# Routing tokens to experts in four groups of blocks instead of once, in a fused Mamba-and-MoE kernel

## The chip, the cores and the metric

The kernel runs on one core of a Trainium2 chip. The metric is the device time of one execution, in microseconds (us); lower is better. The core has a matrix engine (TensorE, PE in the profile), three engines for elementwise work (VectorE or DVE, ScalarE or ACT, GpSimd or POOL), and a synchronisation engine (SyncE or SP) whose queue issues most of the transfers. Each engine works through its own list of instructions strictly in order and waits on semaphores for the others.

## The reference

For x of shape 2 x 2048 x 256 (4096 tokens) the reference computes `x + s * silu(m)`, where `xn = layernorm(x)`:

```
s = mamba block of xn:
    xz = rmsnorm(xn) @ in_proj.T ; xp, z = split(xz)
    xc = silu(causal_conv4(xp))                      # 512 channels
    dt, B, C = parts of xc @ x_proj.T                # 16 states
    h[t] = h[t-1] * exp(dt*A) + dt*xc*B ;  y = sum_states(h*C) + xc*D
    s1 = xn + (y * silu(z)) @ out_proj.T
    s  = s1 + silu(rmsnorm(s1) @ w1.T) @ w2.T        # dense MLP
m = mixture of 8 experts on xn, the best 2 of each token:
    gate = softmax(xn @ gate_w + gate_b); top-2
    m = sum over 2 of gate_k * (relu(xn @ w1[e] + b1[e]) @ w2[e] + b2[e])
```

All of it is float32. The two best experts of a token are known only from the data, so tokens must be sorted to experts at run time.

## The kernel before

The 4096 tokens are cut into 8 blocks of 512 (`NBLK`), a block into 4 rows of 128 tokens (`J`), so that there are `NI` = 32 rows of tokens. The opening of the kernel goes over all blocks; after it one long loop runs the scan, and all other work is drawn into that loop.

**Opening.** `moments(b)` takes means and variances of a block on VectorE (L215, L216). `factors(g)` turns those of a pair of blocks (`GB` = 2) into scales with a ping-pong between VectorE and ScalarE (L193 to L233). `norm(b)` forms `xr` (for the gate and the mamba block) on ScalarE (L243), transposes it on TensorE (L258), and forms `xn`, the rows that the experts need, half on VectorE (L262) and half on ScalarE (L267). `logits(b)` copies the transposed block out of PSUM, one half on ScalarE (L278) and one on VectorE (L279), stores it to DRAM, and multiplies with the gate's weights (L287) into `lgp`. The loop issues norm(b) ahead of logits(b-1).

`gate_and_route()` then runs once, for all 32 rows: on VectorE it scales the logits (L309), picks the two best experts (L319 to L329), counts with two matmuls how many tokens go to each expert ahead of each token (L348, L350), and computes for each token and choice a slot, that is a row in the DRAM buffer `xs_d`, where each expert begins at a multiple of 256 rows (L384 to L386). It also finds for each of the 39 tiles of 256 slots (`NTILE`) which expert owns it (`expert_of`, L396). After it 64 indirect transfers issued by GpSimd scatter the rows of xn to their slots (L1019). Between two of them stands a small copy on ScalarE into the tile `turn` (L1030). `xs_d` was filled with zeros by one transfer of 9,984 KB near the start (L186), since a tile may be only partly used.

`front(c)` makes the inputs of the scan for block c: projection on TensorE (`px`, L474), convolution taps and silu (ScalarE L484 to L507, VectorE L499 and L512), projection to dt, B and C (L520, L537), softplus for dt. B and C go to DRAM (`bcd`, L527) and are loaded back broadcast over all partitions (`load_bc`, L613). The tiles of B and C take over the buffers of x and of xn, so a C load waits for the scatters of one block. front(0) runs in the opening.

**Main loop.** It has 256 steps: block c, group d of 128 channels, pair g of states. In a step VectorE multiplies `b` (L1193) and makes two scans (L1197), ScalarE makes the exponentials for two steps ahead (L1088), GpSimd multiplies the last step's `h` by C (L1129), and TensorE adds `h` into `y` (L1101). There are five `h` buffers. Generators with the other work are drawn on in each step, in a fixed order of preference: the z gate, the output projection, front of the next block (`chain`), and the experts and dense MLP (`side`), which are the largest part of TensorE's work. The experts start at step 4.

An expert tile loads its rows from `xs_d` (L836), its weights by the expert's number, read into a register of SP (L826), and runs two layers (L756, L768). It stores its results to `ys_d` under the same slots (L871). The dense MLP for 256 tokens gathers the two results of each token back with four indirect transfers (L941 and its surroundings in `gather`).

Everything is issued in the order in which the Python code reaches it. No scheduler reorders it.

Of the kernel before, what the change touches and what calls it, by code (L numbers as in the profile page):

```python
# [9 lines left out]
F32 = mybir.dt.float32  # L10
# [21 lines left out]
NSLOT = NTILE * TS  # L32
NCEIL = NT // TS
LN_EPS = 1e-05
# [12 lines left out]
def kernel(  # L47
# [91 lines left out]
    one = rows.tile([P, NE * NI], F32, tag="xs", name="one")  # L139
    nc.gpsimd.memset(one, 1.0)  # L140
# [23 lines left out]
    for d in range(ND):  # L164
# [11 lines left out]
    expert_of = keep.tile([P, NTILE], mybir.dt.int32, tag="expert_of", name="expert_of")  # L176
    xnd = [spill.tile([P, J, DM], F32, tag=f"xnd{b}", name=f"xnd{b}") for b in range(NBLK)]
# [3 lines left out]
    ys_d = spill.tile([NSLOT, DM], F32, tag="ys_d", name="ys_d")  # L181


    zeros = rows.tile([P, NSLOT // P * DM // 64], F32, tag="yk", name="zeros")
    nc.gpsimd.memset(zeros, 0.0)
    nc.sync.dma_start(  # L186
        xs_d.rearrange("(p r) d -> p (r d)", p=P).rearrange("p (o n) -> p o n", o=64),
        zeros.unsqueeze(1).to_broadcast([P, 64, NSLOT // P * DM // 64]),
    )
# [20 lines left out]
    GB = 2  # L210

# [81 lines left out]
    def gate_and_route():  # L293
        def tmp3(name, shape=None):
            return hpool.tile(shape or [P, NI, NE], F32, tag="hid", name=name)

        scratch = rows.tile([P, JS * DM], F32, tag="x1", name="scratch")
        used = [0]

        def cols(name, n):  # L300
            used[0] += n
            return scratch[:, used[0] - n : used[0]]

        sh = [P, NI, NE]
        sel = [
            rows.tile(sh, F32, tag="yk", name=f"sel{k}") for k in range(TOPK)
        ]
        lg = rows.tile(sh, F32, tag="ys", name="lg")
        nc.vector.tensor_tensor(lg, lgp, unr.unsqueeze(2).to_broadcast(sh), ALU.mult)  # L309
        nc.vector.tensor_tensor(  # L310
            lg, lg, gb_sb.unsqueeze(1).to_broadcast(sh), ALU.add
        )
        top = [cols(f"top{k}", NI) for k in range(TOPK)]
        pr = tmp3("pr")
        for k in range(TOPK):
            left = lg
            if k:
                left = tmp3("left")
                nc.vector.scalar_tensor_tensor(left, sel[0], -3e38, lg, ALU.mult, ALU.add)  # L319
            nc.vector.tensor_reduce(top[k], left, AX.X, ALU.max)  # L320
            nc.vector.tensor_tensor(
                sel[k], left, top[k].unsqueeze(2).to_broadcast(sh), ALU.is_equal
            )
            nc.vector.tensor_tensor(
                sel[k], sel[k], fore.unsqueeze(1).to_broadcast(sh), ALU.mult
            )
            first = cols(f"first{k}", NI)
            nc.vector.tensor_reduce(first, sel[k], AX.X, ALU.max)
            nc.vector.tensor_tensor(  # L329
                sel[k], sel[k], first.unsqueeze(2).to_broadcast(sh), ALU.is_equal  # L330
            )
        nc.vector.tensor_tensor(
            pr, lg, top[0].unsqueeze(2).to_broadcast(sh), ALU.subtract
        )
        nc.scalar.activation(pr, pr, AF.Exp)
        tot = cols("tot", NI)
        nc.vector.tensor_reduce(tot, pr, AX.X, ALU.add)
        nc.vector.tensor_single_scalar(tot, tot, 2.0, ALU.mult)
        nc.vector.reciprocal(prob[:, 0, :], tot)
        nc.vector.tensor_sub(top[1], top[1], top[0])  # L340
        nc.scalar.activation(top[1], top[1], AF.Exp)
        nc.vector.tensor_mul(prob[:, 1, :], top[1], prob[:, 0, :])

        mask = tmp3("mask", [P, NE, NI])
        nc.vector.tensor_add(mask.rearrange("p e i -> p i e"), sel[0], sel[1])
        flat = mask.rearrange("p e i -> p (e i)")
        pe = ps_h.tile([P, NE, NI], F32, tag="h", name="pearlier")
        nc.tensor.matmul(pe.rearrange("p e i -> p (e i)"), earlier, flat, start=True, stop=True)  # L348
        pt = ps_h.tile([P, NE, NI], F32, tag="h", name="ptotal")
        nc.tensor.matmul(pt.rearrange("p e i -> p (e i)"), all1, flat, start=True, stop=True)  # L350
        tot_e = tmp3("tot_e", [P, NE, NI])
        nc.scalar.copy(tot_e, pt)

        ahead = tmp3("before_e", [P, NE, NI])
        nc.vector.tensor_tensor_scan(
            ahead.rearrange("p e i -> p (e i)"), one, tot_e.rearrange("p e i -> p (e i)"),
            0.0, ALU.mult, ALU.add,
        )
        nc.vector.tensor_sub(ahead, ahead, tot_e)

        cnt = cols("cnt", NE)
        nc.vector.tensor_reduce(cnt, tot_e, AX.X, ALU.add)
        nc.vector.tensor_single_scalar(cnt, cnt, 1.0 / TS, ALU.mult)
        over = tmp3("over", [P, NE, NCEIL])
        nc.vector.tensor_tensor(
            over, cnt.unsqueeze(2).to_broadcast([P, NE, NCEIL]),
            steps[:, 0:NCEIL].unsqueeze(1).to_broadcast([P, NE, NCEIL]), ALU.is_gt,
        )
        tiles = cols("tiles", NE)
        nc.vector.tensor_reduce(tiles, over, AX.X, ALU.add)  # L370
        upto = cols("upto", NE)
        nc.vector.tensor_tensor_scan(upto, one[:, 0:NE], tiles, 0.0, ALU.mult, ALU.add)
        base = cols("base", NE)
        nc.vector.tensor_sub(base, upto, tiles)
        nc.vector.scalar_tensor_tensor(
            base, base, float(TS), ahead[:, :, 0], ALU.mult, ALU.subtract
        )
        nc.vector.tensor_add(ahead, ahead, pe)
        nc.vector.tensor_tensor(
            ahead, ahead, base.unsqueeze(2).to_broadcast([P, NE, NI]), ALU.add  # L380
        )
        sl = cols("sl", NI)
        for k in range(TOPK):
            nc.vector.tensor_mul(sel[k], sel[k], ahead.rearrange("p e i -> p i e"))  # L384
            nc.vector.tensor_reduce(sl, sel[k], AX.X, ALU.add)
            nc.vector.tensor_copy(slot[:, k, :], sl)  # L386

        done = tmp3("done", [P, NTILE, NE])
        nc.vector.tensor_tensor(
            done, upto.unsqueeze(1).to_broadcast([P, NTILE, NE]),  # L390
            steps.unsqueeze(2).to_broadcast([P, NTILE, NE]), ALU.is_le,
        )
        own = cols("own", NTILE)
        nc.vector.tensor_reduce(own, done, AX.X, ALU.add)
        nc.vector.tensor_scalar_min(own, own, float(NE - 1))
        nc.vector.tensor_copy(expert_of, own)  # L396


# [58 lines left out]
    def bank(tag, shape, name):  # L457
        n = ring(tag, 3 if tag == "h" else 1)
        pool = ps_h if tag == "h" else ps_1
        return pool.tile(shape, F32, tag=tag, name=name), n  # L460

# [355 lines left out]
    class Expert(Ffn):  # L817
# [6 lines left out]
        def begin(self):  # L824
            i = self.i
            e = nc.sync.value_load(expert_of[0:1, i : i + 1], min_val=0, max_val=NE - 1)  # L826
            self.a1 = w1[bass.ds(e, 1)].rearrange("o d f -> (o d) f")
            self.a2 = w2[bass.ds(e, 1)].rearrange("o f d -> (o f) d")
            self.b1 = small.tile([P, NH], F32, tag="b1", name=f"b1_{i}")
            nc.sync.dma_start(self.b1, b1[bass.ds(e, 1)].rearrange("o p c -> (o p) c"))  # L830
            self.e = e

        def rows(self):
# [3 lines left out]
                self.xr, xs_d[ts(i, TS), :].rearrange("(j p) d -> p j d", p=P)  # L837
# [39 lines left out]
    class Mlp(Ffn):  # L877
# [51 lines left out]
        def gather(self):  # L929
# [9 lines left out]
            for j in range(JS):  # L939
                for k in range(TOPK):  # L940
# [3 lines left out]
                            ap=slot[:, k, i0 + j : i0 + j + 1], axis=0  # L944
                        ),
                        bounds_check=NSLOT - 1,
# [59 lines left out]
    for b in range(NBLK + 1):  # L1006
# [6 lines left out]
        if b:  # L1013
            logits(b - 1)
    gate_and_route()
    turn = small.tile([P, 1], F32, tag="turn", name="turn", bufs=1)
    for i in range(NI):
        for k in range(TOPK):
            r = nc.gpsimd.indirect_dma_start(  # L1019
                out=xs_d,  # L1020
                out_offset=bass.IndirectOffsetOnAxis(ap=slot[:, k, i : i + 1], axis=0),
                in_=xns[i // J][:, i % J, :],
                in_offset=None,
                bounds_check=NSLOT - 1,
                oob_is_err=False,
            )

            tc.declare_no_dep(r.ins, group="to_slots", reason="other rows")
            tc.add_to_no_dep_group("to_slots", r.ins)
            nc.scalar.copy(turn, zero3[:, 0:1])  # L1030
    ffns = [Expert(i) for i in range(NTILE)] + [
        Mlp(c, hf) for c in range(NBLK) for hf in range(2)
    ]
    ffns[0].begin()
    for h in range(4):
        ffns[0].load_w1(h)
        ffns[0].load_w2(h)
    for got in front(0):
        if got == "wait":
            tick()  # L1040
# [241 lines left out]
```

## Time and profile before

| quantity | value |
|---|---|
| median of 3 timed runs | 1610.03 us (1606.42 to 1612.15) |
| the profiled execution's own time | 1625.14 us |
| its span in the profile | 1623.4 us |
| mean granted TensorE clock | 0.945 |
| busy: PE, PE weight load | 1427.8 us (88%), 996.2 us (61%) |
| busy: DVE, POOL, ACT | 1276.7 us (79%), 1126.0 us (69%), 872.6 us (54%) |
| moved by transfers | 274.33 MB, mean 169 GB/s |

In a row of the timeline the first two numbers are the start and the duration in us, then come engine, line, operation, the tile written and the tiles read, shapes, and the count of instructions that were merged into the row; in brackets stands how long the engine had been idle before it and what released it. "issue" there means that the profile shows nothing that the engine waited for. SPq and POOLq are the instruction streams of SP and POOL themselves, which issue transfers. In a table of windows each engine has its busy time and, in brackets, its number of instructions; PEclk is the TensorE clock that was granted.

### The profile page before, as it was taken

The page shows a single profiled execution, that of the slowest core. Times are in us where ns is not written, and L with a number is a line of the kernel's source. Part 1 is how long each engine was busy: PE and PEld are TensorE (multiplying, and loading weights), DVE is VectorE, ACT ScalarE, POOL GpSimd, SP SyncE. Part 2 cuts the span into 40 slices and gives each one's busy share as a digit, 9 for nine tenths or more (in the row PEclk, how much of TensorE's full clock was granted, in tenths as well). Part 3 has the DMA queues.
Part 4 walks back from the last instruction along what each step waited for, and adds up shares of the span by engine and source line. Part 5 has one row for each costly group of instructions (what it writes and reads, how often), then busy time and mean ns, then how long its engine had stood idle before and what let it go on. Part 6 is the DMA issues. An engine that isn't in the chain of part 4 may idle for free. (4 is left out here: it accounts for less than half of the span.)

```text
span 1623.4 us, 18334 instructions
## 1 busy us (share of the span) xinstructions
PE 1427.8 (88%) x5266; PEld 996.2 (61%) x5266; DVE 1276.7 (79%) x1380; ACT 872.6 (54%) x1891; POOL 1126.0 (69%) x742
## 2 busy tenths in 40 slices
PE   5751599999999999999999999999898998899867
PEld 4610266776667667765776677667665655567636
DVE  7545577679987998789888987898699977889952
ACT  5463346545665566545655665556554575454423
POOL 0077346676798668956986689669875787677852
PEclk9965799999999999999999999999998979899978
DMA  9665233592449234933494348524772435744322
GB/s 338 256 232 194 91 109 111 152 325 87 137 150 363 71 108 136 334 122 101 144 319 149 94 149 297 180 77 136 224 276 78 132 114 199 244 143 142 93 70 84
DMA packets 209747, 274.33 MB, mean 169 GB/s; under 512 B 21600, under 2 KB 180192, under 8 KB 209648
## 3 DMA queue, kind: packets, MB, share of 16 engines
q1 hardware_dynamic: 203504, 256.39, 48.4%
q0 software_dynamic: 6144, 16.79, 3.0%
q8 instruction: 42, 0.69, 0.2%
q14 instruction: 57, 0.47, 0.1%
HBM read 228.02 MB, written 45.09 MB: 168 GB/s over the span
## 5 line engine op out<-in xcount | busy, mean ns | idle before, releaser
L1129 POOL TENSOR_TENSOR h<-h,C 128x1024 f32<-128x1024 f32 x256 | 608.1, 2378 | 282.8 <-ACT hs L1125 211.9
L1197 DVE TENSOR_TENSOR_SCAN h<-da,hs,b 128x512 f32<-128x512 f32 x384 | 480.8, 1271 | 29.6 <-PE y L1101 6.2
L1088 ACT ACTIVATE da<-dt,a_neg 128x512 f32<-128x512 f32 x512 | 358.5, 718 | 50.8 <-DVE h L1197 50.6
L1101 PE MATMUL y<-h,ident 128*128 128x512 f32 x626 | 316.6, 611 | 33.3 <-POOL h L1129 18.2
L1193 DVE TENSOR_TENSOR b<-du,B 128x1024 f32<-128x1024 f32 x256 | 314.7, 1229 | 6.2
L756 PE MATMUL phe<-xsTe,w_e 128*128 128x256 f32 x1248 | 290.9, 383 | 11.8 <-DVE sz L634 6.0
L768 PE MATMUL poe<-w_e,hide 128*128 128x256 f32 x1248 | 289.6, 382 | 2.8 <-ACT hide L853 2.8
L756 PEld LDWEIGHTS phe<-xsTe,w_e 128*128 128x128 f32 x1248 | 236.9, 191 | 82.9 <-issue 28.2
L768 PEld LDWEIGHTS poe<-w_e,hide 128*128 128x128 f32 x1248 | 236.9, 191 | 66.7 <-issue 30.4
L1131 POOL TENSOR_TENSOR h<-h 128x512 f32<-128x512 f32 x199 | 257.8, 1295 | 15.6
L853 ACT ACTIVATE hide<-phe,b 128x256 f32<-128x256 f32 x312 | 129.7, 468 | 147.9 <-PE phe L756 147.8
L1101 PEld LDWEIGHTS y<-h,ident 128*128 128x128 f32 x626 | 119.3, 197 | 125.9 <-issue 69.6
L1197 DVE TENSOR_TENSOR_SCAN h<-da,b 128x512 f32<-128x512 f32 x128 | 151.9, 1211 | 19.1 <-PE y L1101 11.0
L756 PE MATMUL phm<-xsTm,w_m 128*128 128x256 f32 x512 | 134.2, 418 | 26.5 <-DVE hidm L914 13.7
L756 PEld LDWEIGHTS phm<-xsTm,w_m 128*128 128x128 f32 x512 | 106.2, 210 | 58.7 <-DVE hidm L914 17.0
L1019 POOL DMA_INDIRECT xs_d<-xn,slot x64 | 63.2, 987 | 91.5 <-DVE slot L386 72.3
L768 PE MATMUL pom<-w_m,hidm 128*128 128x256 f32 x512 | 120.4, 386 | 2.3 <-DVE xom L987 2.3
L768 PEld LDWEIGHTS pom<-w_m,hidm 128*128 128x128 f32 x512 | 98.7, 194 | 30.2 <-issue 14.3
L499 DVE SCALAR_TENSOR_TENSOR xc<-px,par_sb,xc 128x512 f32<-128x512 f32 x96 | 71.6, 746 | 29.7 <-ACT xc L491 19.9
L941 POOL DMA_INDIRECT ykm<-ys_d,slot x64 | 64.8, 1012 | 38.7 <-DVE pom L986 18.6
L914 DVE SCALAR_TENSOR_TENSOR hidm<-hidm,phm 128x512 f32<-128x512 f32 x64 | 42.4, 671 | 54.4 <-ACT hidm L912 54.4
L912 ACT ACTIVATE hidm<-phm 128x512 f32<-128x512 f32 x64 | 37.8, 592 | 67.8 <-PE phm L756 64.0
(155 smaller groups left out, 1409.7 us busy)
## 6 DMA issues: line engine op xcount, KB each, us to landing
w_e<-in_w SPq DMA_DIRECT2D x312, 256.0 KB
B<-bcd SPq DMA_DIRECT2D x64, 512.0 KB
C<-bcd SPq DMA_DIRECT2D x64, 512.0 KB
w_m<-in_mlp_w1T SPq DMA_DIRECT2D x64, 256.0 KB
w_m<-in_mlp_w2T SPq DMA_DIRECT2D x64, 256.0 KB
xs_d<-zeros SPq DMA_DIRECT2D x1, 9984.0 KB
xs<-xs_d SPq DMA_DIRECT2D x39, 256.0 KB
ys_d<-ys SPq DMA_DIRECT2D x39, 256.0 KB
```

What stands on the lines that cost most here:

```text
L499: nc.vector.scalar_tensor_tensor(v[:, s : s + T], px, conv_w[:, d, KC - 1 - s : KC - s], v[:, s : s + T], ALU.mult, ALU.add,)
L756: nc.tensor.matmul(ph[:, q, :], self.w1[c0 // 2][:, k, ts(q, P)], self.xT[:, k, :], start=(k == 0), stop=(k == KM - 1),)
L768: nc.tensor.matmul(po[:, j, :], self.hid[c // 2][:, c % 2, ts(j, P)], self.w2[c // 2][:, c % 2, :], start=(c == 0 and j == 0), stop=(c == ...
L853: nc.scalar.activation(hc[:, q, :], ph[:, q, :], AF.Relu, bias=self.b1[:, c0 + q : c0 + q + 1])
L941: nc.gpsimd.indirect_dma_start(out=yk[k][:, j, :], out_offset=None, in_=ys_d, in_offset=bass.IndirectOffsetOnAxis(ap=slot[:, k, i0 + j : i ...
L1019: r = nc.gpsimd.indirect_dma_start(out=xs_d, out_offset=bass.IndirectOffsetOnAxis(ap=slot[:, k, i : i + 1], axis=0), in_=xns[i // J][:, i ...
L1088: nc.scalar.activation(das[n][:, q, :], dts[c, d], AF.Exp, scale=a_neg[:, d, 2 * g + q : 2 * g + q + 1])
L1101: nc.tensor.matmul(ys[c, d], ident, hts[n][:, q, :], start=False, stop=(g == DS // 2 - 1 and q == nq - 1),)
L1129: nc.gpsimd.tensor_tensor(hts[n], hts[n], bct[c, "C", g], ALU.mult)
L1131: nc.gpsimd.tensor_tensor(hts[n][:, 0, :], hts[n][:, 0, :], hts[n][:, 1, :], ALU.add)
L1193: nc.vector.tensor_tensor(inp, dus[c, d].unsqueeze(1).to_broadcast([P, 2, T]), bct[c, "B", g], ALU.mult,)
L1197: nc.vector.tensor_tensor_scan(hts[n][:, q, :], das[n][:, q, :], inp[:, q, :], 0.0 if c % CPB == 0 else hs[c - 1][:, d, 2 * g + q : 2 * g ...
```

## The change

- The gate runs four times, for two blocks (8 rows of tokens) each. `gate(g)` follows logits(2g+1) in the opening's loop, and `scatter(g)` with 16 indirect transfers follows `gate(g)`.
- So that slots can be given before all tokens are counted, each expert has a region of 4352 rows (`CAP`) of its own in `xs_d`, which now has 34,816 rows. `ends` holds the next free row of each expert and is carried from group to group.
- After the last gate `tiles_of_experts()` finds from `ends` which expert owns each of the 39 tiles and at which row of `xs_d` the tile starts (`row_of`). The results in `ys_d` stay compact: `row_y` holds for each token and choice the slot less the gaps between regions, and the gather uses it.
- The zeros for the whole buffer are gone. `fill_up()` writes 256 rows of zeros at the end of each expert's rows, eight transfers on SP whose place is read into a register.
- The small instruction between two scatters is now a memset on GpSimd.
- The order of first loads changes: `xrT[1]`, block 1 of the transposed input, is loaded ahead of the first weights instead of in step 1; the rows of expert tile 0 are loaded ahead of the last two C tiles of block 0; front(1) enters the main loop's list at step 0 instead of step 4.

```diff
+CAP = NT + TS
+NSLOT = NE * CAP
+GB = 2
+GI = GB * T // P
...
-    zeros = rows.tile([P, NSLOT // P * DM // 64], F32, tag="yk", name="zeros")
+    zeros = rows.tile([P, JS, DM], F32, tag="yk", name="zeros")
     nc.gpsimd.memset(zeros, 0.0)
-    nc.sync.dma_start(
-        xs_d.rearrange("(p r) d -> p (r d)", p=P).rearrange("p (o n) -> p o n", o=64),
-        zeros.unsqueeze(1).to_broadcast([P, 64, NSLOT // P * DM // 64]),
-    )
...
+    def gate(g):
+        i = slice(g * GI, (g + 1) * GI)
+        sh = [P, GI, NE]
...
+        vec.tensor_tensor(
+            lg, lgp[:, i, :], unr[:, i].unsqueeze(2).to_broadcast(sh), ALU.mult
+        )
+        vec.tensor_tensor(lg, lg, gb_sb.unsqueeze(1).to_broadcast(sh), ALU.add)
+        for k in range(TOPK):
+            of = lg
+            if k:
+                of = left
+                vec.scalar_tensor_tensor(left, sel[0], -3e38, lg, ALU.mult, ALU.add)
+            vec.tensor_reduce(top[k], of, AX.X, ALU.max)
...
+        vec.tensor_add(mask.rearrange("p e i -> p i e"), sel[0], sel[1])
...
+        nc.tensor.matmul(
+            both[:, 0, :], all1, mask.rearrange("p e i -> p (e i)"), start=True, stop=True
+        )
+        nc.tensor.matmul(
+            both[:, 1, :], earlier, mask.rearrange("p e i -> p (e i)"), start=True, stop=True
+        )
+        vec.tensor_tensor(pr, lg, top[0].unsqueeze(2).to_broadcast(sh), ALU.subtract)
+        vec.tensor_copy(tot_e, both[:, 0, :].rearrange("p (e i) -> p e i", e=NE))
...
+        for k in range(TOPK):
+            vec.tensor_mul(sel[k], sel[k], tot_e.rearrange("p e i -> p i e"))
+            vec.tensor_reduce(slots[:, k, i], sel[k], AX.X, ALU.add)
+            vec.tensor_copy(slot[:, k, i], slots[:, k, i])
+        vec.tensor_add(ends[:, 0, :], ends[:, 0, :], ahead[:, :, GI - 1])
+        nc.scalar.activation(pr, pr, AF.Exp)
+        vec.tensor_sub(top[1], top[1], top[0])
+        nc.scalar.activation(top[1], top[1], AF.Exp)
+        vec.tensor_reduce(tot, pr, AX.X, ALU.add)
+        vec.tensor_single_scalar(tot, tot, 2.0, ALU.mult)
+        vec.reciprocal(prob[:, 0, i], tot)
+        vec.tensor_mul(prob[:, 1, i], top[1], prob[:, 0, i])
...
+    def scatter(g):
+        for i in range(g * GI, (g + 1) * GI):
+            for k in range(TOPK):
+                r = nc.gpsimd.indirect_dma_start(
+                    out=xs_d,
+                    out_offset=bass.IndirectOffsetOnAxis(ap=slot[:, k, i : i + 1], axis=0),
+                    in_=xns[i // J][:, i % J, :],
...
+                to_slots(r.ins)
+                nc.gpsimd.memset(turn, 0.0)
...
+    def fill_up():
+        for e in range(NE):
+            r0 = nc.sync.value_load(end_of[0:1, e : e + 1], min_val=0, max_val=NSLOT - TS)
+            r = nc.sync.dma_start(
+                xs_d[bass.ds(r0, TS), :].rearrange("(j p) d -> p j d", p=P), zeros
+            )
+            to_slots(r.ins)
...
             self.e = e
+            self.row = nc.sync.value_load(
+                row_of[0:1, i : i + 1], min_val=0, max_val=NSLOT - TS
+            )
...
             norm(b)
-        if b:
+        if b % GB == 0 and b >= GB:
             logits(b - 1)
-    gate_and_route()
-    turn = small.tile([P, 1], F32, tag="turn", name="turn", bufs=1)
-    for i in range(NI):
-        for k in range(TOPK):
...
-            nc.scalar.copy(turn, zero3[:, 0:1])
+            gate(b // GB - 1)
+            scatter(b // GB - 1)
+        elif b:
+            logits(b - 1)
+    tiles_of_experts()
     ffns = [Expert(i) for i in range(NTILE)] + [
         Mlp(c, hf) for c in range(NBLK) for hf in range(2)
     ]
+    xrT[1] = rows.tile([P, KM, T], F32, tag="xrT", name="xrTr1")
+    nc.sync.dma_start(xrT[1], xrd[1])
     ffns[0].begin()
     for h in range(4):
         ffns[0].load_w1(h)
         ffns[0].load_w2(h)
+    fill_up()
     for got in front(0):
...
     for which in "BC":
         for g in range(DS // 2):
+            if which == "C" and g == DS // 2 - GB:
+                for _ in ffns[0].rows():
+                    pass
             load_bc(0, g, which)
...
-            if d == 0 and g == 4:
+            if d == 0 and g == (4 if c else 0):
                 chain.append(front(c + 1))
```

`tiles_of_experts()`, left out of the diff above, is 25 instructions on VectorE of 1 to 512 columns.

## The prediction, made before the changed kernel ran

> **What bounds the kernel now.** I first read the table of windows, to see which engine is full where.
>
> ```profile
> core 0: us, PE busy (x) PEld busy (x) DVE busy (x) ACT busy (x) POOL busy (x), PEclk, DMA share, GB/s
> 0.00:200.00 200.00, 103.83 (x287) 63.53 (x288) 108.94 (x260) 91.47 (x230) 83.44 (x90) 0.79 0.64 224
> 200.00:400.00 200.00, 198.21 (x759) 139.50 (x758) 156.63 (x147) 110.95 (x249) 122.59 (x66) 1.00 0.50 159
> ...
> 800.00:1000.00 200.00, 194.36 (x773) 141.51 (x772) 168.34 (x159) 118.96 (x261) 163.78 (x101) 1.00 0.58 190
> ```
>
> From 200 us on TensorE is occupied 93 to 99% of most windows, and the static order there hardly changes. The first 200 us have 96 us without TensorE work. So a change to the opening is worth the shift of the moment at which TensorE becomes full. I mark that moment twice: the first matmul of expert tile 0 (phe, L756) and the b product of scan step 8. Then I read the timeline of the opening, these rows in order of time:
>
> ```profile
> 27.42 2.07 ACT L243 ACTIVATE xr<-xt,stat 128x256 f32<-128x256 f32 x4
> ...
> 29.56 3.16 PE L287 MATMUL lgp<-gw_sb,xrT 128*128 128x8 f32 x14 [1.39 <-DVE xrT L279]
> ...
> 62.65 0.42 DVE L309 TENSOR_TENSOR lg<-lgp,unr 128x256 f32<-128x256 f32 x1 [5.93 <-PE lgp L287]
> ...
> 74.05 14.23 ACT L1030 COPY turn<-zero 128x1 f32<-128x1 f32 x64
> ...
> 82.65 0.97 POOL L1019 DMA_INDIRECT xs_d<-xn,slot  x1 [0.30 <-issue]
> ...
> 89.07 2.33 DVE L499 SCALAR_TENSOR_TENSOR xc<-px,par_sb,xc 128x512 f32<-128x512 f32 x3 [7.13 <-issue]
> ...
> 129.99 1.23 DVE L1193 TENSOR_TENSOR b<-du,B 128x1024 f32<-128x1024 f32 x1
> ...
> 162.15 9.26 POOL L1129 TENSOR_TENSOR h<-h,C 128x1024 f32<-128x1024 f32 x4
> ...
> 170.95 0.42 SPq L1177 DMA_DIRECT2D xrTr<-xrd  x1
> ...
> 179.29 3.70 PE L474 MATMUL px<-xrTr,in_sb 128*128 128x512 f32 x4 [8.77 <-DMA xrTr<-xrd]
> ...
> 184.54 2.33 DVE L499 SCALAR_TENSOR_TENSOR xc<-px,par_sb,xc 128x512 f32<-128x512 f32 x3 [10.62 <-ACT xc L491]
> ...
> 196.03 3.78 PE L756 MATMUL phe<-xsTe,w_e 128*128 128x256 f32 x8 [4.12 <-ACT xsTe L748]
> ...
> 203.66 1.23 DVE L1193 TENSOR_TENSOR b<-du,B 128x1024 f32<-128x1024 f32 x1
> ```
>
> Logits finish at 62.6, routing takes VectorE to 81.9, the taps of front(0) begin at 89.07, and the first scan step at 129.99. GpSimd issues 64 scatters, one each 1.28 us (0.97 + 0.30), from 79.7 to 162.1; only then does it multiply by C, and with five h buffers the scan cannot pass step 4 before. That is the stall which the early scatters attack. After it, px of block 1 waits for xrTr, which SP issues only at 170.95, behind the C loads. The rows of that SP line say why:
>
> ```profile
> L613 SPq EVENT_SEMAPHORE  x39: 13/700/1392, 107.3 to 170.5; - x39
> ```
>
> Most of these semaphore steps of SP last 0.70 us, even where the scatters they name are long done (block 0's were issued by 89), and GpSimd's register moves last 0.70 us in the same stretch against 0.03 at 80 us. After 170 they take 0.01 to 0.03 us. Some of that stall may belong to the recording of the trace: semaphore records are also missing between 86 and 170 us and hardly elsewhere.
>
> [...]0.17 us for 8 columns, 0.42 for 256. So four routings of a quarter each cost far more than one.
>
> **The change part by part.**
>
> *Gate per group.* Each gate has 32 VectorE instructions on 128x64 or smaller. Between 0.17 (8 columns) and 0.42 (256) I estimate 0.22 for 64, plus 0.035 between two: 14 to the mask, 3.6; the two count matmuls on 64 columns, 1.3 (2.2 for 256 in the trace, mask end 71.55 to ptotal end 73.75); 11 to the slots and the top difference, 2.9. That is 7.8 us from logits to the last input of ScalarE, then 1 us of tail. Four gates are about 35 us of VectorE against 19.3.
>
> *Where it stands.* In the order of the changed kernel ScalarE has the gate's two Exp ahead of the next block's xr, and VectorE has the gate ahead of the next xn and factors. ScalarE's second Exp waits for the end of the slots. So after logits(1), ending at 29.56+3.16 = 32.72, the gate runs to 40.5 and xr of block 3, at 27.42 before, starts at 40.85: 13.4 us later. Behind it queue xn, the copies, factors and the transposes. Nothing covers this: norm, logits and gate are one chain. The period of a pair of blocks goes from 11.4 (L221 at 20.14 and 31.59) to 24.9. Gates start at 32.7 and 57.7; the third pair has no moments and starts at 81.5; the fourth pair's logits end at 100.6, against 62.6: **+38 us**.
>
> *After the last gate.* 8.7 us of gate and 25 instructions of tiles_of_experts (three on 512 columns at 0.72, four on 312 at 0.51, the rest 0.2 to 0.3: 8.2 us) put the taps at 117.6. The 64 turn copies on ScalarE, 14.23 us up to 88.3, are gone, but what they held (widen) now waits for VectorE instead. Taps to first step took 129.99−89.07 = 40.9 and is unchanged work: first step at **158.5**, 28.5 later.
>
> *Scatters.* With a memset of some 0.1 us each, 1.28 to 1.4 us: groups start at 40.5, 65.4, 89 and about 111, and end at 131 to 134. They then lie wholly ahead of the first step. The gain is the scan stall: steps 0 to 7 run without it. From the b rows a step is 3.70 us (129.99, 133.68); eight are 29.6; three taps with silu 2.94 each, 8.8; four sz 2.5; du 0.7; one wait for px(2) behind the cold matmuls (0.86 us each), 2.6. Step 8 begins at **202.8**, phe near 196.
>
> *xrT[1] early, C loads after the scatters.* The 8.77 us wait of px goes; the next late thing is the VectorE chain just summed. The xs load of tile 0 waits for the last scatter and goes ahead of C6 and C7: both are needed 30 us after the first step, no cost.
>
> *Zero fill.* 9,984 KB go, 8 x 256 KB come. The old one ran beside norms that do not wait for it: no gain. The eight new ones stand on SP after eight weight loads (0.57 us each): each a register load, register steps and an issue, 1.1 us, from 120.5 to about 130. The bcd store behind them is due at 135, and ScalarE's ex of d=1, which reuses the zeros buffer, at 140. Cover is 5 us; if lost, the excess is added one to one, 0 to 8.
>
> *Compact results, row_of.* One more 0.28 us register load on SP per tile, beside a full TensorE: nothing. front(1) three steps earlier: nothing by itself, its DVE work is in the sum.
>
> **The sum.** Against the profiled execution (1625.14, span 1623.4) step 8 moves from 203.66 to 202.8: −0.9, about 1624. But the timed median, 1610.03, is 15.1 lower. If SP's stall is not in timed runs, the old opening is faster there: the last C load follows the last scatter (162.1[...]), xrTr lands near 168, y of steps 0 and 1 keep TensorE to 171.4, px to 173.2, widen 1.6: taps at 174.8 instead of 184.54. Step 8 follows 19.1 later (203.66−184.54): 193.9. The change then loses 202.8−193.9 = 8.9: **1619**. I take this value because the 15.1 us need a place, and 9.7 of them fit here; the other end is −0.9.
>
> **Rivals.** *A, the likeliest, 0.57:* as summed, 1613 to 1625. *B, no change, 0.20:* the stall of SP and GpSimd is in the timed runs too; the trace of before then counts in full, and the change gives 1609, within 5. For it: the waits are real rows; against: the 15 us. *C, faster, 0.12:* the middle gates fit into idle time. For it: VectorE is busy 35 of the first 60 us. Against: the two Exp in ScalarE's order. The break-even is a first step at 149, when a gate delays the next block by 10.2 us instead of 13.4; with 8 us, step 8 comes at 187: 1603; with all hidden, 1580. *D, much slower, 0.11:* C loads take 7 us each also without scatters beside them; then step 7 waits for C7 until 210, 10 more: about 1630. Against it: the later B and C loads, 314 to 351, show no such steps.
>
> **The numbers.** A measurement here tells about 0.3%, 4.8 us. Slower is D and nearly all of A, 0.65; within, most of B and A's low edge, 0.21; faster, C and B's edge, 0.14. The range runs from C's upper part to the start of D.
>
> **What would show it.** Right: the logits (L296) end near 100 us, gates 25 us apart, ScalarE's xr of blocks 3, 5 and 7 right after a gate's Exp, first b product near 158 and step 8 near 203, GpSimd idle from 133 to 163; a profiled execution that is about as long as before's while the timed runs are longer. Wrong: a first step before 149 (C), C loads 7 us apart (D), or SP held by the fills beyond 135.

## The result, and the profile after

The changed kernel takes 1615.54 us (median of 6 runs, 1613.72 to 1616.69), the kernel before 1609.92 us (6 runs, 1606.02 to 1612.15). The ratio is 1.0038 with a 95% interval of 1.0023 to 1.0053: slower by about 6 us, just outside the 0.3% that were named as the limit of the measurement. The profiled execution of the changed kernel took 1615.90 us (span 1614.2). That is like its timed runs, while the first profile of the kernel before, 1625.14, was not like its own; experiment 3 returns to this.

The table of windows after, with the same columns as before:

```profile
core 0: us, PE busy (x) PEld busy (x) DVE busy (x) ACT busy (x) POOL busy (x), PEclk, DMA share, GB/s
0.00:200.00 200.00, 117.33 (x327) 71.05 (x328) 133.64 (x379) 84.39 (x180) 91.15 (x158) 0.88 0.53 186
200.00:400.00 200.00, 197.40 (x750) 137.68 (x749) 154.15 (x146) 109.97 (x247) 126.28 (x68) 1.00 0.50 159
```

TensorE is busy 197 of the 200 us after 200, as before (198). In the first 200 us VectorE has 379 instructions instead of 260 (269 in a second profile of the kernel before). The timeline of the opening after, the rows that answer to those of before, VectorE, ScalarE, GpSimd, SP and TensorE in order of time:

```profile
32.84 0.23 DVE L381 TENSOR_TENSOR halves<-lgp,unr 128x64 f32<-128x64 f32 x1 [3.25 <-PE lgp L296]
...
40.85 0.21 ACT L424 ACTIVATE scratch<-scratch 128x8 f32<-128x8 f32 x1 [3.93 <-DVE scratch L423]
40.96 2.06 ACT L252 ACTIVATE xr<-xt,stat 128x256 f32<-128x256 f32 x4
...
100.01 0.22 DVE L381 TENSOR_TENSOR halves<-lgp,unr 128x64 f32<-128x64 f32 x1 [6.06 <-PE lgp L296]
...
115.80 2.32 DVE L559 SCALAR_TENSOR_TENSOR xc<-px,par_sb,xc 128x512 f32<-128x512 f32 x3
...
121.15 9.33 SPq L517 DMA_DIRECT2D xs_d<-zeros  x8
...
133.67 0.34 SPq L587 DMA_DIRECT2D bcd<-xd  x1
135.30 4.18 SPq L673 DMA_DIRECT2D B<-bcd  x8
139.84 8.10 SPq L673 DMA_DIRECT2D C<-bcd  x6
...
155.21 1.23 DVE L1250 TENSOR_TENSOR b<-du,B 128x1024 f32<-128x1024 f32 x1
...
159.18 2.35 POOL L1186 TENSOR_TENSOR h<-h,C 128x1024 f32<-128x1024 f32 x1 [29.96 <-DMA b<-in_b]
...
188.43 6.56 PE L816 MATMUL phe<-xsTe,w_e 128*128 128x256 f32 x16 [4.20 <-ACT xsTe L808]
...
196.23 1.23 DVE L1250 TENSOR_TENSOR b<-du,B 128x1024 f32<-128x1024 f32 x1
```

The gates stand at 32.84 to 100.01, where the kernel before had one at 62.65. ScalarE's xr of block 3 follows the gate's second Exp at once, 13.5 us later than before. GpSimd has sent its last scatter at 129 and idles 29.96 us until the first product with C: the old stall is gone, and it has become idle time, because the first scan step has moved from 129.99 to 155.21. The fills end before the store of bcd, and the C loads follow each other at some 1.35 us.

### The profile page after: what moved, and what is told of

Its sections match the earlier page's. It is cut to its first block, busy times and chain, and to the rows that moved or that the text cites. A ratio compares the mean times of both kernels' runs of the same rounds, so it can differ in the third digit from the quotient of the medians.

```text
span 1614.2 us, 18732 instructions
## 1 busy us (share of the span) xinstructions
PE 1426.4 (88%) x5278; PEld 992.3 (61%) x5278; DVE 1295.4 (80%) x1492; ACT 861.2 (53%) x1832; POOL 1134.3 (70%) x809
## 5 line engine op out<-in xcount | busy, mean ns | idle before, releaser
L816 PE MATMUL phm<-xsTm,w_m 128*128 128x256 f32 x512 | 126.1, 399 | 18.7 <-DVE hidm L977 15.1
L816 PEld LDWEIGHTS phm<-xsTm,w_m 128*128 128x128 f32 x512 | 101.3, 200 | 49.1 <-DVE hidm L977 19.5
L1004 POOL DMA_INDIRECT ykm<-ys_d,row_y x64 | 64.9, 1014 | 34.0 <-issue 16.0
```

The source lines that it names most:

```text
L816: nc.tensor.matmul(ph[:, q, :], self.w1[c0 // 2][:, k, ts(q, P)], self.xT[:, k, :], start=(k == 0), stop=(k == KM - 1),)
L1004: nc.gpsimd.indirect_dma_start(out=yk[k][:, j, :], out_offset=None, in_=ys_d, in_offset=bass.IndirectOffsetOnAxis(ap=row_y[:, k, i0 + j : ...
```

## The experiments

The set in which a kernel ran turned out to matter more than the change: the kernel before itself took 1611.53 to 1622.05 us in the four, and the change is worth 6. There are four sets below, each on another chip and at another time, each with the kernel before beside it; two kernels are compared only within a set. In what follows "late semaphores" names what the first profile of before showed: waits that end long after what they wait for (SP's semaphore steps at the loads of B and C lasted 700 ns, median, though block 0's scatters had been issued by 89 us), and no landing recorded for any of the 64 scatters.

### 1. The place of the gate, the number of groups, all gates at the end

Three forms of the changed kernel. The first issues each gate behind the next norm and the next logits, the second does so with two groups of four blocks, the third issues all four gates after the loop.

```diff
 # e1: gate one block later          (e2: the same with GR = 4 in place of GB, GI = GR * T // P)
-        if b % GB == 0 and b >= GB:
-            logits(b - 1)
-            gate(b // GB - 1)
-            scatter(b // GB - 1)
-        elif b:
-            logits(b - 1)
+        if b:
+            logits(b - 1)
+        if b % GB == 1 and b > GB:
+            gate(b // GB - 1)
+            scatter(b // GB - 1)
+    gate(NBLK // GB - 1)
+    scatter(NBLK // GB - 1)
 # e3: in the loop the logits alone, as in e1; after it
...
+    for g in range(NBLK // GB):
+        gate(g)
+        scatter(g)
```

> The changed kernel with each gate and its scatters issued after the next block's norm and logits (gate(0) after logits(2), and so on; the last after the loop). Theory 1 (a gate costs so much because it stands ahead of the next norm on ScalarE and VectorE): xr of block 3 starts near 27.5 us again instead of 40.96, a pair of blocks takes about 20 us instead of 25 (11.4 of norm and logits and 8.7 of gate on VectorE), the last gate starts near 88, first step near 143 instead of 155.2, time 12 us below the changed kernel: about 1603. Theory 2 (VectorE's sum of work sets the opening and the place of the gate doesn't matter): last gate still near 100, time within 3 us of 1615.5.

> The changed kernel with two groups of four blocks instead of four of two, gates again behind the next norm and logits. Theory 1: a gate with 128 columns costs about 10.5 us instead of 8.7, but there are only two, and only one stands in the loop: the last gate starts near 72, taps near 92, first step near 132; scatters end near 137, so that GpSimd is free about when it is needed; step 8 near 175 instead of 196.2, time about 1595 to 1600, below both kernels. Theory 2 (what the changed kernel loses lies outside the opening: register loads, fills, compact rows): step 8 comes early as above, but the time stays above 1606.

> The changed kernel with all four gates and scatters after the loop of norms, where the kernel before has its one routing. Theory 1 (the norm chain is only long because of the gates in it; and a profiled execution is longer than a timed one where scatters run beside the loads of B and C): logits end near 62.6 as before, four gates take 35 us, first step near 146, scatters run from 71 to about 155 beside B and C loads; time about 1609; the steps of 0.70 us on SP are back, and the profiled execution is 5 to 15 us above the timed median. Theory 2 (the steps of 0.70 us are in every execution): profiled and timed agree within 3 us, and the time is 1615 or more.

Measured: 1644.1, 1644.0 and 1648.1 us, ratios 1.0149 (1.0127 to 1.017), 1.0138 (1.0118 to 1.0158) and 1.0159 (1.0143 to 1.0175), beside a kernel before of 1622.05. Only theory 2 of the third kernel fits, that profiled and timed agree and the time is above 1615; no expectation named a time near 1644. The time of before was itself 12 us above that of the result. The timelines of ScalarE, VectorE and TensorE of the second kernel (e2) say why:

```profile
94.54 0.58 ACT L288 COPY xrT<-pt 128x512 f32<-128x512 f32 x1 [23.22 <-issue]
...
95.18 0.59 PE L297 MATMUL lgp<-gw_sb,xrT 128*128 128x8 f32 x2 [18.64 <-issue]
...
102.90 0.69 DVE L289 COPY xrT<-pt 128x512 f32<-128x512 f32 x1 [30.85 <-remote]
```

The two copies wait for results of TensorE and VectorE that the same trace shows ready by 76.5 us; they start 18 and 26 us after. From 58 to 103 us the scatters of the first group run. SP steps slowly too: its eight weight loads, issued within some 5 us in the changed kernel, are spread from 125 to 139 us here, so fills, bcd and B loads are late as well, and the first step starts at 182.86.

In the third kernel (e3) the norms are over before the scatters begin; there it is the last gate that stretches. From its timeline of VectorE:

```profile
96.47 0.22 DVE L390 TENSOR_REDUCE scratch<-halves 128x8 f32<-128x64 f32 x1 [1.18 <-DVE halves L389]
97.19 0.22 DVE L391 TENSOR_TENSOR halves<-halves,scratch 128x64 f32<-128x64 f32 x1 [0.49 <-DVE scratch L390]
97.88 0.22 DVE L392 TENSOR_TENSOR halves<-halves,fore 128x64 f32<-128x64 f32 x1 [0.46 <-DVE halves L391]
99.28 0.22 DVE L393 TENSOR_REDUCE scratch<-halves 128x8 f32<-128x64 f32 x1 [1.18 <-DVE halves L392]
```

VectorE waits 0.5 to 1.2 us for its own last result, where these operations follow each other every 0.26 us in the last gate of the changed kernel's first profile. From the start of the last gate to the taps of front(0) it takes 48.4 us here and 32.8 in e1, against 15.8 there. The profiled executions (1643.2, 1644.0, 1647.3) agree with the timed runs, so the time is not one that only a single profile shows.

### 2. Half of the scatters

The kernel before with every second row of tokens left unscattered.

```diff
-    for i in range(NI):
+    for i in range(0, NI, 2):
```

> The kernel before with 32 of its 64 scatters (those of every second row of tokens left out, so half of the rows stay zero; the work on them is the same). This prices the scan's wait for the scatters. Theory 1 (in timed runs step 8 of the kernel before lies near 190.6, since its profile has a stall of 13 us of its own): scatters end near 121, first step stays near 130, step 8 near 173, time 1610 - 17 = about 1593. Theory 2 (step 8 lies at 203.7 in timed runs as well): 1610 - 30 = about 1580. If the scatters were hidden: 1610.

Measured, in the same set as the three above: 1586.1 us, ratio 0.9771 (0.9758 to 0.9785), 36 us less. Step 8 starts at 165.0 instead of 203.7 of the first profile. Some 6 us of it my expectation had forgotten: half of the turn copies on ScalarE go as well, and the first step starts at 122.9 instead of 128.6 to 130. The rest prices the wait for the scatters, with late semaphores included. The theories counted from 1610; within this set the 30 us that are left are those of theory 2, so the late semaphores are in its timed runs too.

### 3. The kernel before, the changed kernel and two of the forms again

> The kernel before, unchanged, profiled again. In the first profile SP and GpSimd stepped at 0.70 us from 109 to 170 us and the semaphore records of the scatters were missing; the three kernels of the last job, which scatter later, showed the same and TensorE idle up to 23 us with nothing to wait for, and the kernel before took 1622 us beside them instead of 1610. Theory A (a late delivery of semaphores while scatters run, which a chip has or has not, in profiled and timed executions alike): either the steps are there, step 8 starts near 203 and the time is 1620 to 1626, or they are absent, step 8 starts near 190 and the time is about 1610. Theory B (only the recording stretches the profiled execution): the steps are there and the time is 10 to 15 us above the timed runs beside it. Theory C (the steps come from what the kernel does): the steps are there in every run of this kernel, 1622 to 1626.

> The changed kernel again. Theory A: without the late semaphores 1614 to 1617, first step near 155; with them its scatters lie from 40 on beside the whole opening, so each gate and norm is held as in the kernels of the last job: 1635 to 1645 beside 1622 of before. Theory C: the changed kernel's spacing of the scatters avoids the stall: 1614 to 1617 also beside a kernel before of 1622.

> The changed kernel with each gate behind the next norm and logits, again. Theory A: without late semaphores the place of the gate is seen: xr of block 3 near 27.5, the last gate near 88, first step near 143, about 1603; with them 1644 again. Theory C: 1644 in any case.

> Two groups of four blocks with the gate behind the next norm and logits, again. Theory A: without late semaphores the last gate starts near 75, first step near 133, scatters end near 140, step 8 near 177, about 1595 to 1600, below both kernels; with them 1644 again. Theory C: 1644 in any case.

This set came to another chip, and there the late semaphores are absent. SP's semaphore steps at the loads of B and C in the second profile of the kernel before (e5; shortest, median and longest in ns, first and last start in us):

```profile
L613 SPq EVENT_SEMAPHORE  x39: 17/28/28, 107.3 to 163.5; - x39
```

And the issues of its scatters between 40 and 165 us, with their count and median us to landing:

```profile
xs_d<-xn,slot POOLq DMA_INDIRECT x64, 3.2
```

The same program had a median of 700 ns there in its first profile, and no landing. That trace lacks records, too: between 86 and 170 us it holds 149 of semaphore updates, the second one 1544. In this set's profiles of the late gate (e7) and of two groups (e8) 8 and 24 of the 64 scatters have no recorded landing either, though SP's steps at these loads have a median of 28 ns; so landings that are missing in part are no sign of late semaphores.

The opening of the kernel before without late semaphores, from the timelines of VectorE, SP, GpSimd and TensorE:

```profile
113.44 50.43 SPq L613 DMA_DIRECT2D C<-bcd  x8
...
128.55 1.23 DVE L1193 TENSOR_TENSOR b<-du,B 128x1024 f32<-128x1024 f32 x1
...
162.01 9.26 POOL L1129 TENSOR_TENSOR h<-h,C 128x1024 f32<-128x1024 f32 x4
...
163.93 0.42 SPq L1177 DMA_DIRECT2D xrTr<-xrd  x1
...
173.48 2.33 DVE L499 SCALAR_TENSOR_TENSOR xc<-px,par_sb,xc 128x512 f32<-128x512 f32 x3 [3.94 <-ACT xc L491]
...
184.97 3.78 PE L756 MATMUL phe<-xsTe,w_e 128*128 128x256 f32 x8 [4.13 <-ACT xsTe L748]
...
192.59 1.23 DVE L1193 TENSOR_TENSOR b<-du,B 128x1024 f32<-128x1024 f32 x1
```

GpSimd is still held by the scatters until 162.01, but xrTr is issued at 163.93 instead of 170.95 and lands 5.5 us later, at 169.4 (168 was the author's estimate), and step 8 starts at 192.59 instead of 203.66. This execution took 1607.37 us; before's timed runs in this set have a median of 1611.53. Step 8 comes 11.1 us earlier than in the first profile, and the median is 10.5 us below that of the first set.

The changed kernel took 1617.56 us (16 runs, 1612.16 to 1624.50), ratio 1.0039 (1.0026 to 1.0053), the same as in the result; its gates, first step (155.16) and step 8 (196.09) stand where the first profile has them. Theory A holds, for both kernels. Theory C falls: the same late-gate kernel took 1644 us in the first set and took 1620.3 here. Theory B, that only a recorded execution is stretched, falls for the sets, since before's timed runs were 1622 in the first and 1611 in this one. The first profile of before, 1625.14 beside timed runs of 1606 to 1612, still looks like it; on which chip each of these was taken is not on record. Each timed run here comes with its span, so whether recording plays a part in those too is open. Chip and moment changed together, so which of them decides is open as well.

The late gate (e7) took 1620.3 us, ratio 1.0057 (1.0039 to 1.0075): no gain, against my 1603. From its timelines of ScalarE and VectorE:

```profile
27.57 2.07 ACT L252 ACTIVATE xr<-xt,stat 128x256 f32<-128x256 f32 x4
...
37.90 0.22 DVE L381 TENSOR_TENSOR halves<-lgp,unr 128x64 f32<-128x64 f32 x1 [6.09 <-PE lgp L296]
...
64.28 0.22 DVE L381 TENSOR_TENSOR halves<-lgp,unr 128x64 f32<-128x64 f32 x1 [6.09 <-PE lgp L296]
...
101.86 0.22 DVE L381 TENSOR_TENSOR halves<-lgp,unr 128x64 f32<-128x64 f32 x1 [3.25 <-PE lgp L296]
```

The xr of block 3 is back at 27.57, so nothing holds it on ScalarE. Yet the first gates stand 25 to 26 us apart and the last one starts at 101.86. The first two gates now wait 6.09 us for the logits that were issued just ahead of them, though they use older ones, and a gate then stands on VectorE ahead of the factors of the next pair: in this trace they start at 46.63, behind the first gate. The wait has only been exchanged.

Two groups (e8) took 1597.26 us, ratio 0.9908 (0.9894 to 0.9922), 14 us below the kernel before and 20 below the changed one, as expected, though the last gate starts 5 us later than forecast. From its timelines of VectorE, GpSimd and TensorE:

```profile
79.92 0.29 DVE L382 TENSOR_TENSOR halves<-lgp,unr 128x128 f32<-128x128 f32 x1 [5.93 <-PE lgp L297]
...
97.64 2.32 DVE L560 SCALAR_TENSOR_TENSOR xc<-px,par_sb,xc 128x512 f32<-128x512 f32 x3
...
137.01 1.23 DVE L1252 TENSOR_TENSOR b<-du,B 128x1024 f32<-128x1024 f32 x1
...
141.09 2.38 POOL L1188 TENSOR_TENSOR h<-h,C 128x1024 f32<-128x1024 f32 x1
...
170.22 5.41 PE L817 MATMUL phe<-xsTe,w_e 128*128 128x256 f32 x16 [4.21 <-ACT xsTe L809]
...
177.54 1.23 DVE L1252 TENSOR_TENSOR b<-du,B 128x1024 f32<-128x1024 f32 x1
```

An operation on 128 columns takes 0.29 us against 0.23 on 64, and the first gate takes 10.9 us on VectorE against 8.8 in the changed kernel, so half as many gates cost little more each. One gate instead of three stands inside the loop. The last one starts 20 us earlier than in the changed kernel, and the scatters end at 141, just as the first product with C is due: neither engine waits long for the other. It beats both kernels, but only without late semaphores; in the first set the same kernel was 22 us slower than before. There (e2) step 8 starts at 223.89, 46.4 us later than here, and the time is 46.8 us longer: what late semaphores cost is in the opening.

### 4. What in a gate holds the next block

Two groups with the gate ahead of the next norm again (e9), the changed kernel with the gate's tail done once (e10), and half of the scatters once more (e11).

```diff
 # e9: two groups (GR = 4), the gate where the changed kernel has it
...
+        if b:
+            logits(b - 1)
+        if b % GR == 0 and b:
+            gate(b // GR - 1)
+            scatter(b // GR - 1)
 # e10: in gate(g), the differences go to lgp and prob; one tail for all rows after front(0)
-        vec.tensor_tensor(pr, lg, top[0].unsqueeze(2).to_broadcast(sh), ALU.subtract)
+        vec.tensor_tensor(lgp[:, i, :], lg, top[0].unsqueeze(2).to_broadcast(sh), ALU.subtract)
...
-        nc.scalar.activation(pr, pr, AF.Exp)
-        vec.tensor_sub(top[1], top[1], top[0])
-        nc.scalar.activation(top[1], top[1], AF.Exp)
-        vec.tensor_reduce(tot, pr, AX.X, ALU.add)
...
+        vec.tensor_sub(prob[:, 1, i], top[1], top[0])
+    def weights():
+        tot = scratch[:, 0:NI]
+        nc.scalar.activation(lgp, lgp, AF.Exp)
+        nc.scalar.activation(prob[:, 1, :], prob[:, 1, :], AF.Exp)
+        nc.vector.tensor_reduce(tot, lgp, AX.X, ALU.add)
...
```

> Two groups of four blocks as in the run before, but each gate where the changed kernel has it, right behind the logits and ahead of the next norm. If the number of gates decides: gate(0) runs from 44 to 55, block 5 waits for it as block 3 did in the changed kernel, and the last gate starts near 80 as with the later place (79.9): about 1595 to 1600. If the place decides (a gate ahead of the next norm holds it by 13 us or more, one behind it does not): last gate near 90, about 1607 or more.

> The changed kernel with the gate's tail (two Exp on ScalarE and five small operations on VectorE, four times) done once for all 32 rows after front(0); everything up to the slots stays where it is. If ScalarE's order is what holds the next block (the two Exp ahead of xr): xr of block 3 starts near 27.6 again, a middle gate delays the chain by 8 us instead of 13.4, the last gate starts near 86 and the time is about 1602. If VectorE's own order holds it anyway (xn and the copy of the transposed block stand behind the gate there): 2 to 3 us less per middle gate and 1 us of tail each, last gate near 92, first step near 146, about 1607.

> The kernel before with half of its scatters left out (those of every second row of tokens), again: the price of the wait for the scatters. Without late semaphores step 8 starts near 165 instead of 192.6 and the time is 27 us less, about 1584 beside 1611; if the scan's wait were worth nothing, 1611. With late semaphores 1586 beside 1622 as before.

This set, on a third chip, has late semaphores (the eight B loads of e11 are issued within 15.40 us, those of e5 within 4.55): before 1621.22, the three kernels 1643.5 (ratio 1.0138, 1.0115 to 1.0162), 1645.5 (1.0159, 1.0137 to 1.0181) and 1584.7 (0.9774, 0.9747 to 0.9801). The first two times therefore decide nothing. What precedes the delays in the traces can be read. Two rows of ScalarE's timeline in e9, then one in e8:

```profile
54.32 2.06 ACT L253 ACTIVATE xr<-xt,stat 128x256 f32<-128x256 f32 x4
...
62.47 2.08 ACT L253 ACTIVATE xr<-xt,stat 128x256 f32<-128x256 f32 x4 [1.32 <-issue]
...
64.29 2.08 ACT L253 ACTIVATE xr<-xt,stat 128x256 f32<-128x256 f32 x4 [1.50 <-DVE stat L241]
```

In e9 the gate holds xr of block 5 until 54.32 and xr of block 6 starts at 62.47; in e8, with the gate behind norm and logits, xr of block 6 starts at 64.29. So the place makes less than 2 us, and of the sign opposite to what I had named for it; the scatters had run for 9 us by then, which can only have delayed e9. From ScalarE's timeline in e10, and last the row of the changed kernel (e6) that answers to the second:

```profile
27.58 2.08 ACT L252 ACTIVATE xr<-xt,stat 128x256 f32<-128x256 f32 x4
...
46.22 2.07 ACT L252 ACTIVATE xr<-xt,stat 128x256 f32<-128x256 f32 x4 [1.44 <-DVE stat L240]
...
49.22 2.07 ACT L252 ACTIVATE xr<-xt,stat 128x256 f32<-128x256 f32 x4 [1.32 <-DVE stat L240]
```

Without the Exp xr of block 3 starts at 27.58 as in the kernel before, but xr of block 4 only at 46.22, against 49.22 in the changed kernel (e6). Of a middle gate's cost some 3.0 us come from ScalarE's part and the tail (more, if the 6 us of scatters ahead of it delayed e10); the rest is VectorE's own queue. The half scatters gave the same 36 us as in experiment 2, as expected with late semaphores; without them, where 27 us were expected, they did not run.

### 5. The new place of front(1)

```diff
-            if d == 0 and g == (4 if c else 0):
+            if d == 0 and g == 4:
                 chain.append(front(c + 1))
```

> Two groups of four blocks with the gate behind the next norm and logits (1597 us on a chip without late semaphores, 1644 on one with them), and front(1) entering the main loop's list at step 4 again, the one line of the change that alters TensorE's order after the opening. In all runs so far step 64 to 192 took 675 to 676 us with front(1) at step 0 and 681 to 682 with it at step 4, and step 192 to 224 took 209 to 213 against 199 to 203. If that line is the cause, both stretches turn back to 681 and 201 here. The line was costed at nothing: then the time stays within 4 us of 1597 (or of 1644), since the last stretch, step 224 to the end, takes the rest back (234 to 241 with the old order, 232 to 235 with the new). If the loss of 10 us between 192 and 224 is not given back, the time falls to about 1590 (or 1637). If the stretches don't turn back, another part of the change makes them.

By its times this set has late semaphores again: 1643.16 us, ratio 1.0127 (1.0108 to 1.0146), beside 1620.59; the same kernel with front(1) at step 0 (e2) took 1644.04 under like conditions. From the starts of the b products in the traces:

| us | step 8 to 64 | 64 to 192 | 192 to 224 | 224 to end |
|---|---|---|---|---|
| before, second profile (e5) | 299.3 | 681.1 | 198.7 | 233.9 |
| changed kernel, second profile (e6) | 298.9 | 674.7 | 212.5 | 234.1 |
| two groups, front(1) at step 0 (e2) | 300.1 | 675.7 | 209.8 | 232.8 |
| two groups, front(1) at step 4 (e12) | 299.2 | 677.8 | 202.7 | 236.7 |

The stretch from 192 to 224 turns back nearly in full: that line alone moves time between stretches of the main loop, all the way to its end. For 64 to 192 it can't be told. Over all traces this stretch takes 674.7 to 677.2 us with front(1) at step 0 and 678.0 to 681.6 at step 4, wider than my expectation said, and e12 lies between the two. The sum hardly moves: 1118.3 us from step 64 to the end in e2, 1117.2 in e12, one execution each.

## Why the prediction was right, and where its sizes were off

**What bounds the kernel** held: without late semaphores TensorE is busy 197 of the 200 us after 200 with either kernel (169 to 196 in the later windows of the changed one), and the change acts by the moment at which that begins. Two groups show it best: step 8 comes 18.6 us earlier than in the changed kernel (e6), and the time is 20.3 us less. With late semaphores and the changed order the moment itself comes later, with expert tile 0 at 216.09 to 219.20 us in e1, e2 and e3.

**The sign and the mechanism** held. The gates lengthen the opening, the scan stall goes, and the first is a little more than the second. Compared without late semaphores (e5 against the profile after), step 8 moves from 192.59 to 196.23, 3.6 us, and the first matmul of expert tile 0 from 184.97 to 188.43, 3.5 us.

**Which loss was forecast, which measured.** 8.9 us were forecast and 5.6 timed. Three terms of the sum were off. Steps 0 to 8 take 41.0 us, not 44.3: px(2) of block 1, put at 2.6 of these, makes nobody wait (in the first profile of before the first four px of block 1 took 3.70 us, from 179 to 183 us at a granted clock of 0.52; px(2) takes 1.88 us here, at 178.47, where the clock from 170 to 183 us was 0.99). The first step starts at 155.21, not 158.5: the taps stand at 115.80 instead of 117.6, since the last gate starts 0.6 us earlier and `tiles_of_experts()` takes 7.2 us instead of 8.2, and taps to first step are 39.4 us, not 40.9; in e5 they are 39.5 too, so the 40.9 of the first profile held 1.4 us of late semaphores. And step 8 of the kernel before, put at 193.9 without the stall, is at 192.59. That makes 8.9 − 3.3 − 3.3 + 1.3 = 3.6. The 2 us between this and the timed 5.6 (interval 3.7 to 8.5) are not located: from step 8 to the end of the span single executions took 1413.0 (e5), 1419.7 (before's first profile), 1418.0 and 1420.2 (the changed kernel), a wider spread than what is sought.

**Gate per group.** Right: 0.22 to 0.23 us for 64 columns, and 8.0 us from the gate's start at 32.84 to ScalarE's second Exp at 40.85, against 7.8. The four starts were forecast as 32.7, 57.7, 81.5 and 100.6; they are 32.84, 58.05, 81.21 and 100.01.

**Where it stands.** The number was right (xr of block 3 at 40.96, forecast 40.85), and so were the signs it named: xr of blocks 3, 5 and 7 start 0.1 us after the start of a gate's second Exp. The reason was right only by half. The prediction put the two Exp in ScalarE's order first. Experiments 3 and 4 show that with them out of the way, or the gate behind the norm, xr of block 3 returns to 27.6 and the next pair gains 3.0 us or nothing. What remains is VectorE's own order: the factors of the next pair stand behind the gate there, wherever it is put, and in the changed kernel xn and the copy of the transposed block as well. The number of gates is what counts: e7 and e8 have the gate in the same place and differ by it, 1620.3 against 1597.3 us.

**Scatters, loads, fills.** The scatters keep the pitch of 1.28 us and end at 129.1, not 131 to 134. The eight fills run from 121.15 to 130.5, ahead of the bcd store at 133.67: the cover held, with 3 us left. The B loads are issued within 4.2 us and the C loads 1.35 us apart, so rival D falls. front(1) at step 0 moves time about; it was costed at nothing, and e2 and e12 differ by 1 us from step 64 on.

**Against the profiled execution** the sum failed. About 1624 was forecast, 1615.90 came, because the sum took the first profile of before as its base. That profile had late semaphores, the one after had none. The prediction saw that 15 us of it needed a place and took the value without them, which gave the right side. In part that was luck: the timed runs of the result (1609.92 us for the kernel before) met no late semaphores, and the prediction couldn't know it. Its suspicion that the stall belongs to the recording was not confirmed: in the three sets in which it appeared, the timed runs were longer as well (1620.59 to 1622.05 us for the kernel before, against 1611.53). With late semaphores rival B expected no change. The changed kernel itself was never run in that condition; e3 and e10, its nearest relations, lost 1.6% there, with the last gate and `tiles_of_experts()` beside the scatters: 48.4 and 34.0 us from the last gate to the taps instead of 15.8. What delays the semaphores is open: nine in ten of the records of semaphore updates of that stretch are missing as well (149 against 1544), and no run isolates the cause.

**Rival C** needed a first step before 149. Four gates, wherever they stood, left it at 155 to 157 without late semaphores; two have room for it (137.01). Of the first 60 us before the change VectorE is busy 36, not 35; that VectorE is idle for the other 24 did not help, since the gate and the next factors follow each other on it.

## What to carry to other kernels

Splitting a step to start its consumer early pays only until the consumer is ready in time. Count what each further split adds to the queue of the engine that carries the chain: four gates freed GpSimd 30 us before it was needed and put the first step 27 us later, two freed it just in time. Moving such a step in the program helped nothing where the engine that executes it also carries the chain (e7 1620.3 us, the changed kernel beside it 1617.56); look for the engine whose queue it lengthens, not for the engine that waits. And where a profiled execution is longer than its timed runs (1625.14 against 1609.92 us here), profile the unchanged kernel again, on another chip if there is one, before building a sum on its waits: here the second profile had steps of 28 ns where the first had 700.

## What was not expected of the hardware

The same program has two modes here, and they differ by more than noise. In three of the four sets of experiments the kernel before took 1620.59 to 1622.05 us instead of 1611.53. The traces of two of these sets show waits that ended late while indirect transfers ran, the third (e12) is put with them for its times: in e2 two copies started 18 and 26 us after their inputs were ready, and no transfer issued from 40 to 165 us has a recorded landing; in e11 the eight B loads were issued within 15.40 us instead of 4.55; in the first profile of before SP's semaphore steps took 700 ns instead of 28 (medians). Each set was on another chip, but also at another time, so that the chip is the cause is not shown. Two groups are 0.9% faster than the kernel before in one mode and 1.4% slower in the other. From one mode to the other the kernel before loses 10.5 us, the late gate 23.8 and two groups 46.8.
